# A second level of Strassen inside three products of q, k and v

## The chip, the cores and the metric

The kernel runs on one NeuronCore of a Trainium2 chip. The metric is device time in microseconds (us) of one execution; the times below are medians over runs. TensorE multiplies matrices into PSUM (eight banks of 128 partitions by 512 float32), VectorE and ScalarE read PSUM, GpSimd works on SBUF alone, and transfers are queued on SyncE.

## The reference

Two layers over 64 graphs of 256 nodes with 512 features, with one shared 256x256 adjacency. All values are float32.

```
h = relu(layernorm(x));   x = x + (adj @ h) @ W0 + b0                  # layer 0
h = relu(layernorm(x))                                                  # layer 1: 8 heads of 64
q, k, v = h @ Wq + bq, h @ Wk + bk, h @ Wv + bv
a = softmax(q k^T / 8 + (1 - adj) * -1e9)
x = x + (a v) @ Wo + bo
```

## The kernel before, in words

Work goes in 32 groups of two batches (512 tokens). A first loop over groups runs layer 0 and leaves the residual and the hidden state in DRAM; a second loop runs layer 1.

Every dense product (W0, Wq, Wk, Wv, Wo) of a group is done by one level of Strassen's algorithm in the Winograd form, with seven block products in place of eight. The two column halves of the operand are the group's two batches. `weight_sums` (L405) makes the sums of weight quarters once, `Halves.sums` (L433) makes the sums of activation quarters (t1 to t4) for each group on GpSimd, `product` (L439) issues one block product, and `project` (L447) the seven of them. A block product is four matmuls of 128x128 weights over 256 columns into one bank; each shows as two TensorE instructions in the profile. `project` keeps a running sum in bank `pa`: a11 b11, then + s2 t2, then + s3 t3. `read` takes the state of a bank out before more is added to it (on ScalarE for q, k and v; for W0 and Wo it is an add on VectorE), and `finish` adds a bank and such a partial result into a target with one VectorE add (`add`, L492). The order of products is a11, a12, s2, s1, s3, a22, s4.

Banks are handed out by hand, first in, first out (`bank`, `give`): a bank that is given back goes to the end of the list of free ones, and whoever takes it waits for its last reader. Partial results u have three buffers in turn (`partial`, L489).

The order of the second loop (from L816) for each group g is: `attend(g, 0)`, `score(g, 1)`, `queries_keys(g+1)`, `attend(g, 1)`, `score(g+1, 0)`, `values(g+1)`, `post(g)`. Each engine takes its instructions in the order in which they are issued. `score` (L684) makes scores for two head groups and two batches: four pairs of banks, which VectorE scales and masks into SBUF (L699, eight instructions); GpSimd subtracts a row maximum (L705), ScalarE takes the exponential (L710), and GpSimd adds keys (L717). `attend` (L719) makes denominators (`pden`) and the weighted values (`pav`, two banks); VectorE takes reciprocals (L743) and, one step later, divides (L750), which frees these two banks. `post` (L661) is the product with Wo; its `read` (L667) and `finish` (L671) add into the residual on VectorE.

Side work is put off with `after(delay, ...)` to later steps; `tick` (called at every `yield` of a running product sequence) issues what is due. So a GpSimd sum given with delay 2 enters GpSimd's queue two products later. `hidden_sums` (L619) does so for t1 to t4 of the hidden state, during `post`.

Of the kernel before, what the change touches and what calls it, by code (L numbers as in the profile page):

```python
# [8 lines left out]
F32 = mybir.dt.float32  # L9
I32 = mybir.dt.int32  # L10
AF = mybir.ActivationFunctionType
ALU = mybir.AluOpType
AX = mybir.AxisListType
P = 128
# [7 lines left out]
def load_weight(nc, pool, w, name):  # L22
    t = pool.tile([P, w.shape[0] // P, w.shape[1]], F32, name=name)
    nc.sync.dma_start(t, w.rearrange("(c p) o -> p c o", p=P))
    return t


def load_row(queue, pool, b, name):
    t = pool.tile([P, b.shape[0]], F32, name=name)
    queue.dma_start(t, bass.AP(tensor=b.tensor, offset=b.offset, ap=[[0, P], [1, b.shape[0]]]))  # L30
    return t
# [167 lines left out]
def kernel(  # L199
# [16 lines left out]
    nc = tc.nc  # L216
    B, N, D = x.shape
    H, HD = 8, D // 8
    DC = D // P
    NT = N // P  # L220
    GB = 2
# [12 lines left out]
    const = main.enter_context(tc.tile_pool(name="const", bufs=1))  # L234
    dram = main.enter_context(tc.tile_pool(name="between", bufs=1, space=bass.MemoryType.DRAM))
    xpool = main.enter_context(tc.tile_pool(name="x", bufs=4))
    act = main.enter_context(tc.tile_pool(name="act", bufs=1))
# [8 lines left out]
    def bank(shape, name):  # L246
        i = free_banks.pop(0)
        t = psum.tile(shape, F32, tag=f"bank{i}", name=name)
        bank_of[id(t)] = (i, t)
        return t  # L250

    def give(t):
        free_banks.append(bank_of.pop(id(t))[0])
# [5 lines left out]
    def after(delay, fn, *args):  # L259
        entered[0] += 1  # L260
        later.append((clock[0] + delay, entered[0], fn, args))
# [8 lines left out]
    X, H0, Q, K, V, OT = {}, {}, {}, {}, {}, {}  # L270
# [18 lines left out]
    def quarter(xt, i, k):  # L289

        return xt[:, k * NT:(k + 1) * NT, i * HF:(i + 1) * HF]
# [11 lines left out]
    b0_r = load_row(nc.scalar, const, b0, "b0_r")  # L303
    w0_sb = load_weight(nc, const, w0, "w0_sb")
# [8 lines left out]
    adjT = const.tile([P, NT, N], F32, name="adjT")  # L313
# [89 lines left out]
    W = {}  # L403
# [16 lines left out]
    class Halves:  # L420

        def __init__(self, name, tokens, which):
            self.tokens = tokens
            self.t = {n: act.tile([P, 2, N], F32, tag=f"{n}{which}", name=f"{n}_{name}")
                      for n in ("t1", "t2", "t3", "t4")}

        def operand(self, n, c=slice(0, 2)):
            if n[0] == "t":
                return self.t[n][:, c, :]
            j, k = int(n[1]) - 1, int(n[2]) - 1  # L430
            return self.tokens[k][:, 2 * j:2 * j + 2, :][:, c, :]

        def sums(self, eng, which=("t1", "t2", "t3", "t4"), c=slice(0, 2)):  # L433
            args = {"t1": ("b12", "b11"), "t2": ("b22", "t1"), "t3": ("b22", "b12"), "t4": ("b21", "t2")}
            for n in which:
                p, q = args[n]
                eng.tensor_tensor(self.t[n][:, c, :], self.operand(p, c), self.operand(q, c), op=ALU.subtract)  # L437

    def product(ps, s, a, halves, b, by_token, start=True, stop=True):  # L439
        for m in range(2):  # L440
            for c in range(2):
                w, y = s[a][:, c, :], halves.operand(b, c)
                lhs, rhs = (y[:, m * P:(m + 1) * P], w) if by_token else (w[:, m * P:(m + 1) * P], y)
                nc.tensor.matmul(ps[:, m, :], lhs, rhs, start=(start and m + c == 0), stop=(c == 1),  # L444
                                 skip_group_check=True)

    def project(s, halves, by_token, name, read, finish, first_half_first=False):  # L447


        def new(n):  # L450
            return bank([P, 2, N], f"{name}{n}")
        pa = new("a")
        product(pa, s, "a11", halves, "b11", by_token, stop=False)
        u1 = read(pa, 1)
        yield
        if first_half_first:
            pc = new("c")
            product(pc, s, "s1", halves, "t1", by_token, stop=False)
            c22 = read(pc, 0)
            yield  # L460
        pb = new("b")
        product(pb, s, "a12", halves, "b21", by_token)
        finish(pb, u1, 0, 0)
        give(pb)
        yield
        product(pa, s, "s2", halves, "t2", by_token, start=False, stop=False)
        u2 = read(pa, 2)
        yield
        if not first_half_first:
            pc = new("c")  # L470
            product(pc, s, "s1", halves, "t1", by_token, stop=False)
            c22 = read(pc, 0)
            yield
        product(pa, s, "s3", halves, "t3", by_token, start=False)
        u3 = read(pa, 3)
        finish(pa, c22, 1, 1)
        give(pa)
        yield
        pd = new("d")
        product(pd, s, "a22", halves, "t4", by_token)  # L480
        finish(pd, u3, 1, 0)
        give(pd)
        yield
        product(pc, s, "s4", halves, "b22", by_token, start=False)
        finish(pc, u2, 0, 1)
        give(pc)
        yield

    def partial(name, n):  # L489
        return tmp.tile([P, 2, N], F32, tag="u", name=f"u{n}_{name}")  # L490

    def add(o, ps, u):  # L492
        nc.vector.tensor_tensor(o, ps, u, op=ALU.add)  # L493
# [113 lines left out]
    H1T, HH, HO = {}, {}, {}  # L607
# [11 lines left out]
    def hidden_sums(g, *steps):  # L619

        HH[g] = Halves(f"h_{g}", [H1T[g][:, k] for k in range(GB)], 0 if g else 1)
        for step, n in zip(steps, ("t1", "t2", "t3", "t4")):
            after(step, HH[g].sums, nc.gpsimd, (n,))

    def queries_keys(g):

        for n, store in (("q", Q), ("k", K)):
            store[g] = {}
            bias = L1[n][1]

            def read(ps, m):
                u = partial(f"{n}_{g}", m)
                for c in range(2):
                    f = 2 * (m in (0, 3)) + c
                    nc.scalar.activation(u[:, c, :], ps[:, c, :], AF.Identity, bias=bias[:, f:f + 1])
                return u

            def finish(ps, u, i, k):
                o = store[g][i, k] = act.tile([P, 2, N], F32, tag=f"{n}{i}{k}", name=f"{n}_{g}_{i}{k}")
                add(o, ps, u)  # L640

            yield from project(W[n], HH[g], False, f"{n}_{g}", read, finish)

    def values(g):
        v = act.tile([P, HQ, GB, NT, HF], F32, tag="yT0", name=f"v_{g}")
        V[g] = {(i, k): v[:, i, k] for i in range(HQ) for k in range(GB)}

        def read(ps, m):
            u = partial(f"v_{g}", m)
            nc.scalar.copy(u, ps)  # L650
            return u

        def finish(ps, u, i, k):
            add(V[g][i, k], ps, u)

        yield from project(W["v"], HH.pop(g), True, f"v_{g}", read, finish)

    def quarter_of(batch, i):
        return batch.rearrange("(t p) d -> p t d", p=P)[:, :, i * HF:(i + 1) * HF]

    def post(g):  # L661

        xt = X.pop(g)
        halves = HO.pop(g)
        done = []

        def read(ps, n):  # L667
            o = quarter(xt, *RESIDUAL[n])
            add(o, ps, o)

        def finish(ps, u, i, k):  # L671
            o = quarter(xt, i, k)
            add(o, ps, o)
            done.append(k)
            if g == NG - 1:
                nc.sync.dma_start(quarter_of(out[g * GB + k], i), o)
            elif done.count(k) == 2:
                nc.sync.dma_start(out[g * GB + k].rearrange("(t p) d -> p t d", p=P), xt[:, k * NT:(k + 1) * NT, :])

        yield from project(W["o"], halves, True, f"o_{g}", read, finish, first_half_first=g == NG - 1)  # L680
# [82 lines left out]
    def run(gen, steps=99):  # L763

        for _ in zip(range(steps), gen):
            tick()
# [46 lines left out]
    run(steps)  # L813
    hidden_sums(1, 1, 2, 8, 9)
    run(values(0))
    for g in range(NG):  # L816
        attend(g, 0)
        load_residual(g)
        if g + 2 < NG:
            load_hidden(g + 2)  # L820
        score(g, 1, 5)
        tick()
        for t in range(T):
            after(9 + t, lambda t, xt: nc.gpsimd.tensor_tensor(xt[:, t, :], xt[:, t, :], L1["o"][1], op=ALU.add), t, X[g])  # L824
        if g + 1 < NG:
            run(queries_keys(g + 1))
        else:
            run(post(g - 1))
        attend(g, 1)
        if g + 1 < NG:  # L830
            score(g + 1, 0, 5)
            tick()
            run(values(g + 1))
            if g + 2 < NG:
                hidden_sums(g + 2, 2, 3, 4, 5)
                run(post(g))
    tick()
    last = post(NG - 1)
# [45 lines left out]
```

## Time and profile before

| what | value |
|---|---|
| median of 3 runs | 2727.9 us (2727.74 to 2728.13) |
| profiled span | 2725.3 us |
| VectorE's masked scores (L699), 512 | 312.1 us busy, 683 ns each |
| GpSimd's subtraction (L705), 254 | 593.7 us busy, 2373 ns each |
| VectorE's reciprocals (L743), 256 | 216.8 us busy, 909 ns each |
| mean granted TensorE clock | 0.998 of full speed |

In the profile, PE is TensorE's matmuls and PEld its weight loads, DVE is VectorE, ACT is ScalarE, POOL is GpSimd. A line of a timeline gives the start and the length in us, the engine, the line of the kernel, the instruction with its output and inputs, its shape and how many are merged into the line; in brackets stands how long the engine had been idle and who ended that. Durations of neighbours can overlap: an engine takes the next instruction before the last one's results are out.

### The profile page before, as it was taken

Reading aid. Unit: us, or ns where it says so; the run is one execution under the profiler, and the core shown is the slowest. Engines: PE = TensorE matmul, PEld = TensorE weight load, DVE = VectorE, ACT = ScalarE, POOL = GpSimd, SP = SyncE. Lnnn points to the kernel's source line nnn. Section 1 sums busy time; section 2 is a strip of 40 time slices with the busy share of each in tenths; the row PEclk is TensorE's granted clock in tenths of the full one; section 3 lists DMA queues with packets and bytes.
Section 4 is the critical chain, followed back from the end, with each engine's and each line's share of the span. In section 5 each row is a group of like instructions: output and inputs, shape, how many; then the busy total and the mean of one; then the engine's idle time right before and its main releaser. Section 6 shows DMA issues by size and latency. Waiting matters only on the chain.

```text
span 2725.3 us, 43511 instructions
## 1 busy us (share of the span) xinstructions
PE 2699.5 (99%) x17172; PEld 2252.1 (83%) x17172; DVE 1539.6 (56%) x2781; ACT 874.2 (32%) x1537; POOL 1823.1 (67%) x1426
## 2 busy tenths in 40 slices
PE   8999999999999999999999999999999999999998
PEld 7888888888788888888888888888888888888886
DVE  7877778775444444455554444454555445444556
ACT  3434343443233223222233322222223332223222
POOL 6777776764666666666666666666666666666665
PEclk9999999999999999999999999999999999999999
DMA  7776666664111111111111111111222111111110
GB/s 187 188 193 163 162 168 169 165 153 93 47 47 47 47 47 47 47 47 47 47 47 47 47 47 47 47 47 56 61 62 57 48 47 47 47 47 47 47 47 32
DMA packets 281023, 210.50 MB, mean 77 GB/s; under 512 B 145904, under 2 KB 212976, under 8 KB 280816
## 3 DMA queue, kind: packets, MB, share of 16 engines
q1 hardware_dynamic: 280352, 207.15, 29.2%
q8 instruction: 138, 2.26, 0.4%
q10 hardware_dynamic: 464, 0.52, 0.1%
q14 instruction: 69, 0.57, 0.1%
HBM read 106.96 MB, written 100.66 MB: 76 GB/s over the span
## 4 chain that ended last, share of the span: by engine, by line
PE 98%; POOL 1%; DVE 1%; DMA 0%; issue 0%; ACT 0%; DVEq 0%; ACTq 0%; POOLq 0%
PE sc L694 8%; PE py L539 8%; PE pav L733 8%; PE pden L726 2%; POOL a L705 1%; PE v_31a L444 0%; PE q_31a L444 0%; PE q_27a L444 0%; PE v_22a L444 0%; PE v_18a L444 0%; PE q_18a L444 0%; PE q_14a L444 0%; PE v_9a L444 0%; PE v_5a L444 0%; PE q_5a L444 0%; PE v_30a L444 0%
## 5 line engine op out<-in xcount | busy, mean ns | idle before, releaser
L705 POOL TENSOR_TENSOR a<-a,top 128x1024 f32<-128x1024 f32 x254 | 593.7, 2373 | 699.1 <-DVE a L699 699.1
L699 DVE SCALAR_TENSOR_TENSOR a<-sc,maskT 128x512 f32<-128x512 f32 x512 | 312.1, 683 | 28.5 <-PE sc L694 28.5
L717 POOL TENSOR_TENSOR as<-a 128x512 f32<-128x512 f32 x256 | 317.3, 1277 | 0.7 <-DVE r L575 0.7
L710 ACT ACTIVATE a<-a 128x1024 f32<-128x1024 f32 x256 | 270.8, 1058 | 22.4 <-POOL a L705 22.4
L743 DVE RECIPROCAL den<-den 128x128 f32<-128x128 f32 x256 | 216.8, 909 | 66.9 <-ACT den L740 66.8
L694 PE MATMUL sc<-q,k 64*128 64x256 f32 x2048 | 238.7, 383 | 0.0
L733 PE MATMUL pav<-a,v 128*32 128x256 f32 x4096 | 232.7, 379 | 0.0
L694 PEld LDWEIGHTS sc<-q,k 64*128 64x128 f32 x2048 | 194.4, 187 | 44.9 <-issue 26.3
L539 PE MATMUL py<-adjT,h 128*128 128x256 f32 x1024 | 228.9, 382 | 0.9 <-DVE adjT L325 0.9
L740 ACT ACTIVATE den<-pden 128x512 f32<-128x512 f32 x64 | 38.2, 597 | 581.7 <-PE pden L726 570.6
L539 PEld LDWEIGHTS py<-adjT,h 128*128 128x128 f32 x1024 | 196.1, 192 | 28.7 <-ACT h L514 1.2
L733 PEld LDWEIGHTS pav<-a,v 128*32 128x32 f32 x4096 | 133.1, 110 | 87.9
L569 ACT ACTIVATE h<-x,nb,rs 128x512 f32<-128x512 f32 x128 | 97.1, 806 | 319.0 <-POOL nb L54 319.0
L824 POOL TENSOR_TENSOR x<-x,bo_r 128x512 f32<-128x512 f32 x128 | 159.4, 1283 | 12.9 <-DVE x L493 12.9
L53 POOL TENSOR_TENSOR rs<-rs,mhalf 128x2 f32<-128x2 f32 (+1 forms) x97 | 78.8, 812 | 124.3 <-DVE nb L52 124.2
L518 POOL TENSOR_TENSOR x<-x,b_r 128x512 f32<-128x512 f32 x128 | 159.3, 1280 | 1.0 <-ACT h L514 0.9
L437 POOL TENSOR_TENSOR t_y<-yT,t_y 128x256 f32<-128x256 f32 (+1 forms) x96 | 87.8, 915 | 41.5 <-ACT yT L549 39.0
L752 ACT ACTIVATE den<-den 128x512 f32<-128x512 f32 x64 | 40.3, 630 | 221.5 <-DVE den L743 221.5
L590 DVE BATCH_NORM_STATS2 st<-x 128x6 f32<-128x256 f32 x256 | 96.4, 418 | 4.4
L514 ACT ACTIVATE h<-x,nb,rs 128x512 f32<-128x512 f32 x128 | 93.9, 805 | 10.5 <-POOL nb L54 10.5
L42 DVE BATCH_NORM_STATS2 st<-x 128x6 f32<-128x512 f32 x128 | 85.6, 669 | 7.2 <-DMA x<-in_x_dram 7.2
L437 POOL TENSOR_TENSOR t_y<-yT 128x256 f32<-128x256 f32 (+1 forms) x96 | 87.6, 912 | 2.2 <-ACT yT L549 0.9
(3144 smaller groups left out, 5550.1 us busy)
## 6 DMA issues: line engine op xcount, KB each, us to landing
x<-in_x_dram SPq DMA_DIRECT2D x256, 128.0 KB, 3.5
residual<-x SPq DMA_DIRECT2D x256, 128.0 KB, 2.3
hidden<-r SPq DMA_DIRECT2D x128, 256.0 KB, 4.7
h1T<-hidden SPq DMA_DIRECT2D x64, 512.0 KB, 9.5
x<-residual SPq DMA_DIRECT2D x32, 1024.0 KB, 6.5
out_dram<-x SPq DMA_DIRECT2D x62, 512.0 KB, 3.0
w_sb<-in_L_gnn_weight_dram SPq DMA_DIRECT2D x1, 1024.0 KB, 6.3
wq_sb<-in_L_gnn_Wq_dram SPq DMA_DIRECT2D x1, 1024.0 KB, 6.8
```

The costliest lines, as they stand in the source:

```text
L437: eng.tensor_tensor(self.t[n][:, c, :], self.operand(p, c), self.operand(q, c), op=ALU.subtract)
L518: nc.gpsimd.tensor_tensor(xt[:, t, :], xt[:, t, :], b0_r, op=ALU.add)
L539: nc.tensor.matmul(pss[d][:, b * N:(b + 1) * N], h[:, b * NT + k, d * P:(d + 1) * P], adjT[:, k, :], start=(k == 0), stop=(k == NT - 1))
L569: nc.scalar.activation(h1[:, k * NT + t, :], xt[:, k * NT + t, :], AF.Relu, bias=nb[:, t:t + 1], scale=rs[:, t:t + 1])
L694: nc.tensor.matmul(ps[j][:, kt * N:(kt + 1) * N], k[j * HD:(j + 1) * HD, c, kt * P:(kt + 1) * P], q[j * HD:(j + 1) * HD, c, :], start=True ...
L699: nc.vector.scalar_tensor_tensor(a[:, j * NT:(j + 1) * NT, :].rearrange("p k n -> p (k n)"), ps[j], SCALE, maskT_f, op0=ALU.mult, op1=ALU.add)
L705: nc.gpsimd.tensor_tensor(a, a, top_b, op=ALU.subtract)
L710: nc.scalar.activation(a, a, AF.Exp)
L717: nc.gpsimd.tensor_tensor(AS[c, b], a4[:, :, 0, :], a4[:, :, 1, :], op=ALU.add)
L733: nc.tensor.matmul(po[f][h * 32:(h + 1) * 32, b * N:(b + 1) * N], v[:, k, h * HD + f * 32:h * HD + f * 32 + 32], A[h // 2, b][:, (h % 2) * ...
L743: nc.vector.reciprocal(rden[:, c * P:(c + 1) * P], den[:, c * P:(c + 1) * P])
L824: after(9 + t, lambda t, xt: nc.gpsimd.tensor_tensor(xt[:, t, :], xt[:, t, :], L1["o"][1], op=ALU.add), t, X[g])
```

## The change

From group 4 on, three of the seven block products of each of q, k and v, those whose result is used once only (`a12 b21`, `a22 t4`, `s4 b22`), are themselves done by a second level of the same algorithm: seven matmuls of 128x128 over 128 columns in place of four over 256. It is for fewer TensorE columns per product. Four of the seven go to one quarter of the result each, three or four are needed in several quarters and go to a bank `shared`; VectorE then adds the quarters together (`finish2`). For `s4`, which accumulates onto bank `pc`, the fourth shared product can't go straight into the quarter c22.

The operands' sums come from GpSimd: for the weights once, in the first three groups of the second loop (`block_sums`, into the space of layer 0's weights), for the activations in each group (`block_hidden`, steps 6 and 7 of `post`). The order of products becomes a11, s1, s2, a12, s3, a22, s4.

```diff
+    def product2(own, shared, s, x, by_token, fresh):
+        q = own.rearrange("p m (n k) -> p (m n) k", k=P)
+        c11, c12, c21, c22 = (q[:, i, :] for i in ((0, 2, 1, 3) if by_token else (0, 1, 2, 3)))
+        for o, a, b, start in ((shared[:, 0, :], "a11", "b11", True), (shared[:, 1, :], "s2", "t2", False),
+                               (shared[:, 2, :], "s3", "t3", False),
+                               (c22 if fresh else shared[:, 3, :], "s1", "t1", fresh),
+                               (c11, "a12", "b21", False), (c12, "s4", "b22", False), (c21, "a22", "t4", False)):
...
+            nc.tensor.matmul(o, lhs, rhs, start=start, stop=True, skip_group_check=True)
+
+    def finish2(o, own, shared, u, by_token, fresh):
...
+        add(o, own, u)
+        q = quarters(o)
+        lower = q[:, 1::2, :] if by_token else q[:, 2:4, :]
+        right = q[:, 2:4, :] if by_token else q[:, 1::2, :]
+        add(q, spread(0, 4), q)
+        add(q[:, 1:4, :], spread(1, 3), q[:, 1:4, :])
+        add(lower, spread(2, 2), lower)
+        if fresh:
+            add(right[:, 0, :], quarters(own)[:, 3, :], right[:, 0, :])
+        else:
+            add(right, spread(3, 2), right)
+
+    def project2(n, halves, blocks, by_token, name, read, target):
...
+        def once(own, a, i, k, u, fresh):
+            shared = bank([P, 4, P], f"{name}r")
+            product2(own, shared, W2[n, a], blocks[ONCE[a]], by_token, fresh)
+            finish2(target(i, k), own, shared, u, by_token, fresh)
...
+        pa = new("a")
+        product(pa, s, "a11", halves, "b11", by_token, stop=False)
+        u1 = read(pa, 1)
+        yield
+        pc = new("c")
+        product(pc, s, "s1", halves, "t1", by_token, stop=False)
+        c22 = read(pc, 0)
+        yield
+        product(pa, s, "s2", halves, "t2", by_token, start=False, stop=False)
+        u2 = read(pa, 2)
+        yield
+        once(new("b"), "a12", 0, 0, u1, True)
+        yield
+        product(pa, s, "s3", halves, "t3", by_token, start=False)
+        u3 = read(pa, 3)
+        add(target(1, 1), pa, c22)
+        give(pa)
+        yield
+        once(new("d"), "a22", 1, 0, u3, True)
+        yield
+        once(pc, "s4", 0, 1, u2, False)
+        yield
...
-            yield from project(W[n], HH[g], False, f"{n}_{g}", read, finish)
+            if g < FIRST2:
+                yield from project(W[n], HH[g], False, f"{n}_{g}", read, finish)
+            else:
+                yield from project2(n, HH[g], H2[g], False, f"{n}_{g}", read, target)
...
-        yield from project(W["v"], HH.pop(g), True, f"v_{g}", read, finish)
+        if g < FIRST2:
+            yield from project(W["v"], HH.pop(g), True, f"v_{g}", read, finish)
+        else:
+            yield from project2("v", HH.pop(g), H2.pop(g), True, f"v_{g}", read, lambda i, k: V[g][i, k])
...
+        if g < 3:
+            for i, work in enumerate(block_sums("qkv"[g])):
+                after(4 + i // 2, *work)
...
                 hidden_sums(g + 2, 2, 3, 4, 5)
+                if g + 2 >= FIRST2:
+                    block_hidden(g + 2, 6)
                 run(post(g))
```

More of the change, by code (lines that the diff above doesn't have):

```diff
@@ L487, in project, with block_sums, part @@
         yield
+    ONCE = {"a12": "b21", "a22": "t4", "s4": "b22"}
+    FIRST2 = 4
+    W2, spare = {}, []
+    def block_sums(n):
+        todo = []
+        for a in ONCE:
+            w = W[n][a]
+            def part(i, j):
+                return w[:, j, i * P:(i + 1) * P]
+            s1, s2, s3, s4 = (spare.pop(0) for _ in range(4))
+            W2[n, a] = dict(a11=part(0, 0), a12=part(0, 1), a22=part(1, 1), s1=s1, s2=s2, s3=s3, s4=s4)
+            for o, p, q, op in ((s1, part(1, 0), part(1, 1), ALU.add), (s2, s1, part(0, 0), ALU.subtract),
+                                (s3, part(0, 0), part(1, 0), ALU.subtract), (s4, part(0, 1), s2, ALU.subtract)):
+                todo.append((nc.gpsimd.tensor_tensor, o, p, q, op))
+        return todo
@@ new lines, with __init__, operand, sums @@
+    class Blocks:
+        def __init__(self, x, t):
+            self.x, self.t = x, t
+        def operand(self, n):
+            if n[0] == "t":
+                return self.t[..., {"t1": 0, "t3": 1, "t2": 2, "t4": 3}[n], :]
+            return self.x[..., int(n[1]) - 1, int(n[2]) - 1, :]
+        def sums(self, eng):
+            t, op = self.t, ALU.subtract
+            eng.tensor_tensor(t[..., 0:2, :], self.x[..., :, 1, :], self.x[..., 0, :, :], op=op)
+            eng.tensor_tensor(t[..., 2, :], self.operand("b22"), t[..., 0, :], op=op)
+            eng.tensor_tensor(t[..., 3, :], self.operand("b21"), t[..., 2, :], op=op)
@@ new lines, in product2 @@
+    def product2(own, shared, s, x, by_token, fresh):
[5 more added lines that the diff above has]
+                               (c11, "a12", "b21", False), (c12, "s4", "b22", False), (c21, "a22", "t4", False)):
+            lhs, rhs = s[a], x.operand(b)
+            if by_token:
+                lhs, rhs = rhs, lhs
+            nc.tensor.matmul(o, lhs, rhs, start=start, stop=True, skip_group_check=True)
@@ new lines, in finish2, with quarters, spread @@
+    def finish2(o, own, shared, u, by_token, fresh):
+        def quarters(t):
+            return t.rearrange("p m (n k) -> p (m n) k", k=P)
+        def spread(i, n):
+            return shared[:, i:i + 1, :].to_broadcast([P, n, P])
+        add(o, own, u)
[9 more added lines that the diff above has]
+            add(right, spread(3, 2), right)
@@ new lines, in project2, with new @@
+    def project2(n, halves, blocks, by_token, name, read, target):
+        s = W[n]
+        def new(i):
+            return bank([P, 2, N], f"{name}{i}")
+        def once(own, a, i, k, u, fresh):
+            shared = bank([P, 4, P], f"{name}r")
+            product2(own, shared, W2[n, a], blocks[ONCE[a]], by_token, fresh)
+            finish2(target(i, k), own, shared, u, by_token, fresh)
+            give(own)
+            give(shared)
+        pa = new("a")
[20 more added lines that the diff above has]
+        yield
@@ L623, in hidden_sums, with block_hidden @@
             after(step, HH[g].sums, nc.gpsimd, (n,))
+    H2 = {}
+    def block_hidden(g, step):
+        t = act.tile([P, GB, 4, P], F32, tag="t2", name=f"t2_{g}")
+        t4 = act.tile([P, 4, P], F32, tag="t24", name=f"t24_{g}")
+        x = H1T[g][:, :, 2:4, :].rearrange("p k c (n j) -> p k c n j", j=P)
+        both = Blocks(x, t)
+        last = Blocks(HH[g].t["t4"].rearrange("p c (n j) -> p c n j", j=P), t4)
+        H2[g] = {f"b2{k + 1}": Blocks(x[:, k], t[:, k]) for k in range(GB)}
+        H2[g]["t4"] = last
+        after(step, both.sums, nc.gpsimd)
+        after(step + 1, last.sums, nc.gpsimd)
     def queries_keys(g):
@@ L636, in read, with target @@
                 return u
+            def target(i, k):
+                o = store[g][i, k] = act.tile([P, 2, N], F32, tag=f"{n}{i}{k}", name=f"{n}_{g}_{i}{k}")
+                return o
             def finish(ps, u, i, k):
-                o = store[g][i, k] = act.tile([P, 2, N], F32, tag=f"{n}{i}{k}", name=f"{n}_{g}_{i}{k}")
-                add(o, ps, u)
-            yield from project(W[n], HH[g], False, f"{n}_{g}", read, finish)
+                add(target(i, k), ps, u)
+            if g < FIRST2:
+                yield from project(W[n], HH[g], False, f"{n}_{g}", read, finish)
+            else:
+                yield from project2(n, HH[g], H2[g], False, f"{n}_{g}", read, target)
     def values(g):
@@ L824 @@
             after(9 + t, lambda t, xt: nc.gpsimd.tensor_tensor(xt[:, t, :], xt[:, t, :], L1["o"][1], op=ALU.add), t, X[g])
+        if g == 0:
+            for n, tag in ((4 * DC, "w0_sb"), (4, "w0_s1"), (4, "w0_s2"), (4, "w0_s4"), (4, "adjT"), (4, "b0_r")):
+                t = const.tile([P, n, P], F32, tag=tag, name=f"spare_{tag}")
+                spare.extend(t[:, i, :] for i in range(n))
+        if g < 3:
+            for i, work in enumerate(block_sums("qkv"[g])):
+                after(4 + i // 2, *work)
         if g + 1 < NG:
```

## The prediction, made blind

> **What bounds the kernel now.** I read the page first: engine totals, then the chain that ended last.
>
> ```profile
> PE 2699.5 (99%) x17172; PEld 2252.1 (83%) x17172; DVE 1539.6 (56%) x2781; ACT 874.2 (32%) x1537; POOL 1823.1 (67%) x1426
> ...
> PE 98%; POOL 1%; DVE 1%; DMA 0%; issue 0%; ACT 0%; DVEq 0%; ACTq 0%; POOLq 0%
> ```
>
> TensorE is never idle and carries 98% of the chain. So anything taken from it is worth its full time, as long as nobody else then makes it wait. VectorE is busy for only 56% of the span, but that is an average; I read the stretch where the change puts its work. One group of two batches takes two half-periods of about 32.5 us (attend, score and fourteen products each). In the timeline (start, duration, engine, line, what) TensorE and then VectorE show:
>
> ```profile
> 1514.21 1.89 PE L444 MATMUL o_12c<-wo_s,oT 128*128 128x256 f32 x8
> 1516.03 1.07 PE L726 MATMUL pden<-as,ones 128*32 128x256 f32 x16
> 1516.91 3.64 PE L733 MATMUL pav<-a,v 128*32 128x256 f32 x64
> 1520.48 3.72 PE L694 MATMUL sc<-q,k 64*128 64x256 f32 x32
> 1524.13 1.99 PE L444 MATMUL q_14a<-h1T,wq_sb 128*128 128x256 f32 x8
> 1525.96 1.89 PE L444 MATMUL q_14b<-h1T,wq_sb 128*128 128x256 f32 x8
> 1527.69 1.89 PE L444 MATMUL q_14a<-t_h,wq_s 128*128 128x256 f32 x8
> ```
> ```profile
> 1516.13 0.69 DVE L493 TENSOR_TENSOR x<-o_12c,x 128x512 f32<-128x512 f32 x1 [1.03 <-PE o_12c L444]
> 1517.88 3.39 DVE L743 RECIPROCAL den<-den 128x128 f32<-128x128 f32 x4 [1.06 <-ACT den L740]
> 1521.71 4.88 DVE L699 SCALAR_TENSOR_TENSOR a<-sc,maskT 128x512 f32<-128x512 f32 x8 [0.44 <-PE sc L694]
> 1526.51 1.28 DVE L750 TENSOR_TENSOR oT<-pav,den 128x512 f32<-128x512 f32 x2
> ```
>
> A product is eight TensorE instructions (a float32 matmul is two); products follow each other at 1.73 us, 0.216 us an instruction. VectorE is free of its products when attend begins, starts the reciprocals 1.86 us into it and the eight masked scores (L699) 5.7 us into it. These have only 0.44 us of slack; eight take 4.88 us, so one starts every 0.60 us.
>
> **The Trainium skill.** "TensorE: Matmul & The Clock Gate", LDWEIGHTS, puts a load at columns/1.2 ns, 107 ns for 128. Its Back-to-back issue gap section warns that in load-and-matmul pairs both set the pace (81 ns at 128 columns against 56 alone). The change's 128-column matmuls come nearest to the four transposes in the mask set-up, each with its own 128-column load:
>
> ```profile
> 416.96 0.60 PE L341 MATMUL pm<-ident,adj_sb 128*128 128x128 f32 x4
> 417.39 0.81 PE L539 MATMUL py<-adjT,h 128*128 128x256 f32 x3
> ```
>
> Four instructions of 0.272 us each (the tile's own view) span 0.60 us, so (0.60 - 0.272)/3 = 0.109 us apart, half of the 0.216. So here the load fits under a matmul of 128 columns, just.
>
> "VectorE: DVE Perf Modes", The DRAIN you can't avoid, says that order alone doesn't make a read of the result just written safe; a semaphore is wanted. The trace has such pairs:
>
> ```profile
> 412.59 0.69 DVE L42 BATCH_NORM_STATS2 st<-x 128x6 f32<-128x512 f32 x1
> 413.31 0.18 DVE L43 BATCH_NORM_AGGREGATE mv<-st 128x2 f32<-128x6 f32 x1
> ```
>
> The reader starts 0.03 us after the writer's end, while independent instructions start 0.08 us before it (0.60 apart at 0.69). [...] Length I take from the same page's errata section, (N+151)/0.96 ns: 0.691 for 512 (trace 0.69), so estimates of 0.557 for 384, 0.424 for 256 and 0.291 for 128. "GPSIMD Engine Reference", Specifications, has GpSimd contend with VectorE instructions of two SBUF inputs; the new adds have one input in PSUM, like L493, which holds 0.69 beside a busy GpSimd.
>
> **The change, part by part.** It acts in 28 groups (4 to 31), on three products of each of q, k and v: 252 in all.
>
> TensorE: eight instructions of 256 columns become seven matmuls, 14 instructions, of 128. 8 x 0.216 = 1.727 us become 14 x 0.1092 = 1.529; 0.198 saved. Per group 9 x 0.198 = 1.78 us, in all 50 us. That is the whole gain.
>
> VectorE: one add of 0.69 becomes five adds, each reading what the one before wrote. Fresh bank: 0.69 + 0.69 + 0.557 + 0.424 + 0.291 plus four gaps of 0.034, less 0.084 overlap with the next: F = 2.70 us. For s4 the last add is on 256: 2.84. A whole project2 has 2.70 + 0.60 + 2.70 + 2.84 = 8.85 us of VectorE work where there were about 2.5.
>
> It can't begin before the first once-product ends, for the order puts three plain products ahead. Call that moment 0. TensorE then does s3 (1.73), a22 (3.26), s4 (4.79) and is done. VectorE starts 0.27 later (1527.96 against 1527.69 above), and its inputs are there each time: 0.27 + 2.70 = 2.97; add for (1,1) to 3.58; a22 to 6.28; s4 to 9.12. It ends 4.34 us behind TensorE. After q this costs nothing: three plain products of k follow, VectorE is idle by then and the banks in rotation are free. It costs in two places.
>
> Place A, after k: attend and score follow. Queued behind the last add are the reciprocals, then the eight L699. The reciprocals start 4.34 us into attend, not 1.86; with the 0.44 of slack used up, L699 starts 2.05 us late. Score writes eight banks; three are held by attend until L750 or given back just before, so that its last pair takes the banks of its first. Before, these came free just in time (second L699 ends at 1521.71 + 0.60 + 0.69 = 1523.0; the pair is due at 1523.1). So the 2.05 us go to TensorE. K's last quarter is ready 4.4 us into attend, before score's second pair wants it: no cost there.
>
> Place B, after v: post follows. Its first read (L667) adds bank pa to the residual on VectorE, and s2 accumulates into pa only after that. The read now ends at 9.12 + 0.69 = 9.81; s2 is due at 4.79 + 2 x 1.727 = 8.24, and needs some 0.07 for the semaphore and 0.107 for its load: 9.99. TensorE waits 1.75 us. In group 31 no post follows; attend wants V instead, with about the same wait. Later adds of post catch up, as VectorE has 1 us of idle time at each product there.
>
> GpSimd: block sums per group are one 512-, three 256- and two 128-wide operations: 1.28 + 3 x 0.73 + 2 x about 0.45 (estimate, from 1.28 and 0.73) = 4.4 us. In the half-period with post it ends its hidden sums at 1578.5 and idles for 9.5 us until the next scores: hidden there. The 36 weight-block sums (5.5 us in each of three groups) delay key sums by less than the some 8 us until attend. ScalarE keeps its reads, a step earlier for one; copies wait behind the same exponentials as before. New tiles add no DMA.
>
> Sum per group: 2.05 + 1.75 - 1.78 = 2.02 us; 28 x 2.02 = 56 us, on 2727.9: 2784.
>
> **Rivals.** (1) *Five adds that close up.* If each add starts 0.08 us before the end of the one before, F falls by 4 x 0.118 = 0.47, the lag by 1.42, the waits to 0.63 and 0.33: (0.96 - 1.78) x 28 = -23, 2705, faster. For it: independent adds do so. Against: these depend on each other and the trace holds such pairs apart. (2) *VectorE's lag is hidden altogether*: 50 us saved, 2678, faster. For it: only 56% busy. Against: the slack at A is 0.44 us. (3) *Weight loads become the bound.* At the break-even 1.727/14 = 0.123 us a load nothing is saved on a product; the lag shrinks by 2 x 0.198, waits of 1.65 and 1.35 stay: +84, 2812, slower still. At the 0.142 us that one transpose load lasts: 2.0 us a product, +0.26 each on nine, waits 1.1 and 0.8: +119, 2847. For it: "PEld" is 83% busy, and the skill's 81 against 56. Against: 0.109 in the transposes.
>
> **How the numbers follow.** Main case 0.62, (1) 0.14, (2) 0.10, (3) 0.14. In the main case F is uncertain by about 0.15 us, one more semaphore step or one less per add; three of F in each of two waits and 28 groups make 25 us either way. Faster are (1), (2) and a sliver of the main case: 0.25; slower 0.72; same 0.03. The range leaves out most of (2) and the upper end of (3): 2698 to 2825.
>
> **What would show it.** In the trace after: new matmuls 0.109 us apart; five adds in about 2.8 us; reciprocals some 4.3 us after attend begins; a hole of about 2 us before score's last pair, ended by L699's line, and one of 1.7 us before post's s2, ended by VectorE's read; VectorE near 2050 us busy (252 x about 1.96 = 494 more). I'm wrong if VectorE catches up before attend and post, or if the matmuls come slower than 0.12.

## The result, and the profile after

The changed kernel takes 2771.5 us (median; 2769.2 to 2772.0) where the kernel before takes 2728.0: a ratio of 1.0156, 95% interval 1.0138 to 1.0173. It is slower by 43.5 us; the forecast was slower by 56.

The page of the changed kernel, totals and then the chain that ended last:

```profile
PE 2690.7 (97%) x18684; PEld 2271.7 (82%) x18684; DVE 2002.4 (72%) x3789; ACT 875.6 (32%) x1537; POOL 1961.6 (71%) x1630
...
PE 67%; POOL 17%; DVE 14%; issue 1%; DMA 0%; POOLq 0%; ACT 0%; DVEq 0%; SPq 0%; ACTq 0%
```

TensorE's share of the chain fell from 98% to 67%. VectorE is 463 us busier, 1.84 us for each of the 252 products. The chain also names GpSimd at 17%; whether that is a cause has to be tested. First, the stretch where the forecast put its two waits. A once-product here is one of the three products of q, k or v whose result is used once only, and a hole is a stretch in which TensorE waits. TensorE in the changed kernel, from k's first once-product to post (start, duration, engine, line, what; in brackets idle time and who ended it):

```profile
1554.59 0.38 PE L538 MATMUL k_14r<-h1T,wk_sb 128*128 128x128 f32 x2
...
1556.15 1.89 PE L444 MATMUL k_14a<-t_h,wk_sb 128*128 128x256 f32 x8
...
1561.10 1.07 PE L856 MATMUL pden<-as,ones 128*32 128x256 f32 x16
1561.98 3.64 PE L863 MATMUL pav<-a,v 128*32 128x256 f32 x64
1565.55 2.86 PE L824 MATMUL sc<-q,k 64*128 64x256 f32 x24
1569.03 1.72 PE L824 MATMUL sc<-q,k 64*128 64x256 f32 x8 [0.62 <-DVE a L829]
1570.69 1.99 PE L444 MATMUL v_14a<-wv_sb,h1T 128*128 128x256 f32 x8
...
1584.12 1.89 PE L444 MATMUL o_13b<-wo_sb,oT 128*128 128x256 f32 x8
1587.27 1.97 PE L444 MATMUL o_13a<-wo_s,t_o 128*128 128x256 f32 x8 [1.26 <-DVE x L600]
```

The same places in the kernel before:

```profile
1548.51 1.07 PE L726 MATMUL pden<-as,ones 128*32 128x256 f32 x16
...
1556.61 1.99 PE L444 MATMUL v_14a<-wv_sb,h1T 128*128 128x256 f32 x8
...
1570.53 1.89 PE L444 MATMUL o_13b<-wo_sb,oT 128*128 128x256 f32 x8
1572.26 1.89 PE L444 MATMUL o_13a<-wo_s,t_o 128*128 128x256 f32 x8
```

Both holes are where they were forecast: at score's last eight instructions (place A), ended by VectorE's masked scores, and before post's s2 (place B), ended by VectorE's read. From attend to the first product of v took 1570.69 - 1561.10 = 9.59 us, where the kernel before needs 1556.61 - 1548.51 = 8.10: 1.49 us. Half of that lies before the eight instructions and half among them, where TensorE waits for the second of the two banks that they write. Post's s2 was due 1.73 after 1584.12 and started 1.42 later.

VectorE in the same stretch:

```profile
1556.42 0.69 DVE L600 TENSOR_TENSOR k<-k_14b,u_k 128x512 f32<-128x512 f32 x1 [2.88 <-PE k_14b L538]
1557.15 1.74 DVE L600 TENSOR_TENSOR k<-k_14r,k 128x512 f32<-128x512 f32 x3
1558.81 0.28 DVE L600 TENSOR_TENSOR k<-k_14b,k 128x128 f32<-128x128 f32 x1
1559.00 0.68 DVE L600 TENSOR_TENSOR k<-k_14a,u_k 128x512 f32<-128x512 f32 x1
1559.64 0.69 DVE L600 TENSOR_TENSOR k<-k_14d,u_k 128x512 f32<-128x512 f32 x1
1560.37 1.74 DVE L600 TENSOR_TENSOR k<-k_14r,k 128x512 f32<-128x512 f32 x3
1562.03 0.28 DVE L600 TENSOR_TENSOR k<-k_14d,k 128x128 f32<-128x128 f32 x1
1562.22 0.68 DVE L600 TENSOR_TENSOR k<-k_14c,u_k 128x512 f32<-128x512 f32 x1
1562.94 2.20 DVE L600 TENSOR_TENSOR k<-k_14r,k 128x512 f32<-128x512 f32 x4
1565.06 3.38 DVE L873 RECIPROCAL den<-den 128x128 f32<-128x128 f32 x4
1568.35 4.81 DVE L829 SCALAR_TENSOR_TENSOR a<-sc,maskT 128x512 f32<-128x512 f32 x8
```

From 1556.42 to the end of these lines VectorE waits for nobody. The reciprocals start 3.96 us into attend (before: 1.86), the masked scores 7.25 (before: 5.7).

The distance from one attend to the next gives a balance without any modelling. It is read off the starts of `pden` in TensorE's timeline. Each half-period begins with an attend and a score; one goes on with q and k, the other with v and post, and the latter has both holes.

| kernel | half with q and k, us | half with v and post, us | time, us |
|---|---|---|---|
| before | 32.48 | 32.48 | 2728.0 |
| changed | 31.50 | 34.97 | 2771.5 |
| TensorE's part alone | 31.50 | 31.99 | 2687.0 |
| VectorE's part alone | 32.48 | 35.13 | 2803.4 |
| q only | 31.99 | 32.48 | 2713.1 |
| v only | 32.48 | 33.49 | 2758.1 |
| order of before, second level | 31.50 | 34.97 | 2772.5 |
| order of after, one level | 32.48 | 32.48 | 2728.3 |
| spread once-products | 31.50 | 32.85 | 2711.3 |
| spread, last of k and v at one level | 31.66 | 32.15 | 2697.9 |
| reciprocals late | 31.50 | 33.49 | 2731.1 |
| other order in post | 31.50 | 34.58 | 2761.6 |
| both of these | 31.50 | 33.10 | 2723.3 |
| both, on the kernel before | 32.48 | 33.59 | 2761.3 |

So six second-level products save 0.98 us and three save 0.49, 0.164 each, and the two holes together are 34.97 - 31.99 = 2.98 us (1.49 each; in post 1.42 before s2 and 0.07 in s2 itself, which is followed 1589.07 - 1587.27 = 1.80 us later where 1.73 is usual). 28 x (2.98 - 1.47) = 42 us.

### The profile page after: what moved, and what is told of

Its sections match the earlier page's. It is cut to its first block, busy times and chain, and to the rows that moved or that the text cites. A ratio compares the mean times of both kernels' runs of the same rounds, so it can differ in the third digit from the quotient of the medians.

```text
span 2769.3 us, 47852 instructions
## 1 busy us (share of the span) xinstructions
PE 2690.7 (97%) x18684; PEld 2271.7 (82%) x18684; DVE 2002.4 (72%) x3789; ACT 875.6 (32%) x1537; POOL 1961.6 (71%) x1630
## 4 chain that ended last, share of the span: by engine, by line
PE 67%; POOL 17%; DVE 14%; issue 1%; DMA 0%; POOLq 0%; ACT 0%; DVEq 0%; SPq 0%; ACTq 0%
POOL a L835 10%; DVE k L600 9%; PE py L646 8%; PE sc L824 5%; PE pav L863 4%; POOL as L847 4%; DVE den L873 4%; POOL t_o L437 3%; PE pden L856 1%; DVE a L829 1%; DVE x L600 1%; DVE v L600 0%; PE q_27a L444 0%; PE q_25a L444 0%; PE q_19a L444 0%
## 5 line engine op out<-in xcount | busy, mean ns | idle before, releaser
L824 PE MATMUL sc<-q,k 64*128 64x256 f32 x2048 | 262.8, 387 | 17.4 <-DVE a L829 17.4
L840 ACT ACTIVATE a<-a 128x1024 f32<-128x1024 f32 x256 | 264.6, 1057 | 23.9 <-POOL a L835 23.9
```

What stands on the lines that cost most here:

```text
L824: nc.tensor.matmul(ps[j][:, kt * N:(kt + 1) * N], k[j * HD:(j + 1) * HD, c, kt * P:(kt + 1) * P], q[j * HD:(j + 1) * HD, c, :], start=True ...
L840: nc.scalar.activation(a, a, AF.Exp)
```

## The experiments

The theory is the lag, the time by which VectorE ends its adds after TensorE has gone on to attend or post: TensorE is faster, VectorE isn't done when attend and post begin, and what is queued behind it makes TensorE wait. The rivals are GpSimd (17% of the chain), the order of products, and the narrow matmuls themselves.

**Each engine's part alone.** First the four added adds are left out, so the shared products don't enter the result:

```diff
         add(o, own, u)
...
-        add(q, spread(0, 4), q)
-        add(q[:, 1:4, :], spread(1, 3), q[:, 1:4, :])
-        add(lower, spread(2, 2), lower)
-        if fresh:
-            add(right[:, 0, :], quarters(own)[:, 3, :], right[:, 0, :])
-        else:
-            add(right, spread(3, 2), right)
```

> TensorE's part alone. The changed kernel with the last four of the five adds left out, so that the shared products are computed on TensorE but never enter the result (the output isn't the reference's); GpSimd's block sums and the order of products stay. Lag theory: VectorE again ends 0.6 us after each product, both holes (before score's last pair, before post's third product) are gone, and what is left is nine products a group that are 1.727 - 1.56 = 0.165 us shorter: 2728 - 28 x 9 x 0.165 = 2686 us. Rival, GpSimd: the chain in the changed kernel runs 17% over GpSimd, and its extra sums make the holes; then these stay and the time is near 2771.

Measured: 2687.0 us, ratio 0.9849 (0.9833 to 0.9866), with GpSimd's extra sums all made. TensorE has 98% of the chain again, and no hole is left. So the narrow matmuls and GpSimd's sums cost nothing by themselves, and the saving is real: 41 us.

Then VectorE's adds with TensorE's old products:

```diff
-            shared = bank([P, 4, P], f"{name}r")
-            product2(own, shared, W2[n, a], blocks[ONCE[a]], by_token, fresh)
-            finish2(target(i, k), own, shared, u, by_token, fresh)
+            product(own, s, a, halves, ONCE[a], by_token, start=fresh)
+            finish2(target(i, k), own, own.rearrange("p m (n k) -> p (m n) k", k=P), u, by_token, fresh)
```

> VectorE's part alone. The changed kernel with each once-product made again by four matmuls of 256 columns, followed by the same five adds, which read the product's own bank in place of the shared one (the output isn't the reference's); GpSimd's sums and the order stay. Lag theory: VectorE's 8.9 us from the first once-product run against 3 x 1.727 = 5.2 us of TensorE in place of 4.85, so the lag and each hole shrink by 0.33 us: holes of 1.49 - 0.33 = 1.16 and 1.42 - 0.33 = 1.09 us, nothing saved: 2728 + 28 x 2.25 = 2791 us. Rival, narrow matmuls themselves (their waits, weight loads, banks) cause the loss: near 2728.

Measured: 2803.4 us, ratio 1.0273 (1.0256 to 1.029). The sign and place are as forecast, the size is 12 us above. VectorE's timeline of this run shows why:

```profile
1640.38 0.68 DVE L598 TENSOR_TENSOR k<-k_15a,u_k 128x512 f32<-128x512 f32 x1
1641.18 0.69 DVE L598 TENSOR_TENSOR k<-k_15d,u_k 128x512 f32<-128x512 f32 x1
...
1646.60 3.38 DVE L871 RECIPROCAL den<-den 128x128 f32<-128x128 f32 x4
```

The adds of a22 start 0.80 us after the add before, not 0.64: they wait for their product, which ends later than in the changed kernel. So the lag shrinks by 0.16 us (reciprocals 3.80 us into attend, which began at 1642.80), not by the 0.33 that the slower products would give alone. Holes of 1.49 - 0.16 = 1.33 each make 28 x 2.66 = 74 us; the half-period shows 35.13 - 32.48 = 2.65.

**The order of products.** Once undone at two levels, once alone at one level:

```
project2 of the changed kernel:   a11, s1, s2, a12, s3, a22, s4
second level, order of before:    a11, a12, s2, s1, s3, a22, s4
one level, order of after:        a11, s1, s2, a12, s3, a22, s4
```

> The order of products undone: second level and five adds as in the changed kernel, but products in the order of the kernel before (a11, a12, s2, s1, s3, a22, s4). Lag theory: from the end of s3 VectorE does the add for (1,1), waits for a22 (1.56 + 0.27 = 1.83 us), then 2.58 + 2.84 us, so it ends at 7.25 us against TensorE's 3.12: a lag of 4.13 us where the changed kernel has 4.06. So the order hardly matters: 2770 to 2775 us. Rival, the new order is what hurts: 2728 - 41 = 2687 or at least well below 2760.

> The order of products alone: one level everywhere (four matmuls of 256 columns and one add for each product of q, k and v), in the changed kernel's order, with GpSimd's block sums still made though nobody reads them. Lag theory: VectorE ends about 0.9 us after each product sequence as before, no hole: 2728 us, within 2. Rivals, order or GpSimd's sums cost time by themselves: above 2735.

Measured: 2772.5 us (ratio 1.0161, 1.0144 to 1.0178) and 2728.3 us (ratio 1.0000, 0.9992 to 1.0009). The order chosen neither helps nor hurts; the second run also clears GpSimd's block sums once more.

**Which of q, k and v.**

For q alone, k goes back to one level in `queries_keys` and v in `values`; for v alone, `queries_keys` gets the `if True` and `values` stays as it is. The cut shows the two lines of the first run:

```diff
-            if g < FIRST2:
+            if g < FIRST2 or n == "k":
...
-            if g < FIRST2:
+            if True:
```

> The second level for q alone; k and v at one level in the old order. After q three plain products of k follow, in which VectorE can catch up, and neither attend nor post comes next. Lag theory: no hole, and 28 x 3 x 0.165 = 14 us saved: 2714 us. Rival, loss in proportion to the number of second-level products: 2728 + 43.5 x 3/9 = 2742 us.

> The second level for v alone; q and k at one level. Lag theory: the hole after k is gone, the one in post stays at 1.42 us: 2728 + 28 x (1.42 - 3 x 0.165) = 2754 us. If GpSimd's key sums end that hole (they are later in the changed kernel because score is delayed after k), then it shrinks to nothing here, as score isn't delayed any more: 2714 us. Loss in proportion to products: 2742.

Measured: 2713.1 us (ratio 0.9945, 0.9928 to 0.9961) and 2758.1 us (ratio 1.0108, 1.0091 to 1.0125). The same second level gains 15 us in q and loses 30 in v: what follows decides. TensorE in v alone, at post:

```profile
1645.63 1.89 PE L444 MATMUL o_14b<-wo_sb,oT 128*128 128x256 f32 x8
1648.78 1.97 PE L444 MATMUL o_14a<-wo_s,t_o 128*128 128x256 f32 x8 [1.26 <-DVE x L600]
```

It is the same idle time as in the changed kernel, with score no longer delayed. So the hole in post doesn't come from the one in score.

**Where VectorE's work lies.** The same nine second-level products and all the adds, in another order, so that the adds of a12 lie beside s1 and s2:

```
project2 of the changed kernel:   a11, s1, s2, a12, s3, a22, s4
once-products spread:             a11, a12, s1, s2, s4, s3, a22
```

> The changed kernel with the once-products spread: a11, a12, s1, s2, s4, s3, a22. The adds of a12 lie beside s1 and s2; from the end of s4 VectorE does 0.27 + 2.84 + 0.64 + 2.58 = 6.33 us against TensorE's 1.73 + 1.56 = 3.29, a lag of 3.04 in place of 4.06. Lag theory: holes of 0.47 and 0.40 us, so 2728 + 28 x (0.87 - 1.48) = 2711 us, faster than before. Rival, the work on VectorE as a whole counts, not where it lies: no change, 2771.

And the last product of k and v back at one level:

```diff
-        once(new("d"), "a22", 1, 0, u3, True)
+        if n == "q":
+            once(new("d"), "a22", 1, 0, u3, True)
+        else:
+            pd = new("d")
+            product(pd, s, "a22", halves, "t4", by_token)
+            add(target(1, 0), pd, u3)
+            give(pd)
```

> As the run with spread once-products, but the last product of k and of v (a22) is made at one level again, so that seven of nine products a group have the second level. From the end of s4 VectorE does 0.27 + 2.84 + 0.64 + 0.60 = 4.35 us against TensorE's 3.45: a lag of 0.9 us, as in the kernel before. Lag theory: no hole, 28 x 7 x 0.165 = 32 us saved: 2696 us, below both kernels. If some other cost goes with the second level: above 2728.

Measured: 2711.3 us (ratio 0.9937, 0.992 to 0.9954) and 2697.9 us (ratio 0.989, 0.9874 to 0.9907). Both match, and both beat the kernel before. The first has VectorE just as busy as the changed kernel:

```profile
PE 2678.9 (99%) x18684; PEld 2274.2 (84%) x18684; DVE 2006.3 (74%) x3789; ACT 875.5 (32%) x1537; POOL 1962.0 (72%) x1630
```

VectorE's busy time is unchanged but for 4 us (2006), and 60 us have gone from the kernel's time. In the second, VectorE and then TensorE before and in attend:

```profile
1597.20 2.20 DVE L606 TENSOR_TENSOR k<-k_15r,k 128x512 f32<-128x512 f32 x4
1599.32 0.68 DVE L606 TENSOR_TENSOR k<-k_15a,u_k 128x512 f32<-128x512 f32 x1
1599.92 0.68 DVE L606 TENSOR_TENSOR k<-k_15d,u_k 128x512 f32<-128x512 f32 x1
1601.62 3.39 DVE L879 RECIPROCAL den<-den 128x128 f32<-128x128 f32 x4 [1.02 <-ACT den L876]
```
```profile
1599.76 1.07 PE L862 MATMUL pden<-as,ones 128*32 128x256 f32 x16
1600.64 3.64 PE L869 MATMUL pav<-a,v 128*32 128x256 f32 x64
1604.21 3.72 PE L830 MATMUL sc<-q,k 64*128 64x256 f32 x32
1607.87 1.99 PE L444 MATMUL v_15a<-wv_sb,h1T 128*128 128x256 f32 x8
```

VectorE is idle again for 1.02 us before the reciprocals, which start 1.86 us into attend as before, and attend to v takes 8.11 us. TensorE is back at 98% of the chain. GpSimd does the same work in the same order after score as in the changed kernel, and no hole is left in post: its 17% of the chain was no cause. Nor was a shortage of banks: the bank `shared` is taken for seven of the nine products here too, and both half-periods are shorter by the full 0.164 us for each of them.

**The queue at place A and the read at place B, each by itself.** In the first of these runs the reciprocals go behind the masked scores on VectorE:

```diff
+        late = qd == 1 and g < NG - 1
+        def turn():
+            for c in range(4):
+                nc.vector.reciprocal(rden[:, c * P:(c + 1) * P], den[:, c * P:(c + 1) * P])
+        if not late:
+            turn()
...
         def divide():
+            if late:
+                turn()
...
+            if late:
+                after(5, count)
```

> Place A alone mended, by VectorE's queue. In the changed kernel the reciprocals of attend's second half, 3.3 us between the late adds and the masked scores, are issued after the masked scores, and ScalarE's count on them five steps later. Everything else stays, the lag of 4 us too. If the queue in front of the masked scores makes the hole: they start some 4 us into attend, the hole of 1.49 us before score's last pair goes, the one in post stays: 2771.5 - 28 x 1.49 = 2730 us. If score waits for something else (K's last quarter, GpSimd): no gain.

Measured: 2731.1 us (ratio 1.0012, 1.0003 to 1.002), 40 us gained by a change of order alone. VectorE:

```profile
1612.81 2.20 DVE L600 TENSOR_TENSOR k<-k_15r,k 128x512 f32<-128x512 f32 x4
1616.66 4.88 DVE L829 SCALAR_TENSOR_TENSOR a<-sc,maskT 128x512 f32<-128x512 f32 x8 [1.65 <-PE sc L824]
1621.46 3.38 DVE L876 RECIPROCAL den<-den 128x128 f32<-128x128 f32 x4
```

The lag is still there (attend began at 1610.97, the last add ends 4.0 us later), but the masked scores now wait for score, not score for them. The half-period with v and post is 1.48 us shorter. The hole at A was the queue, not K's last quarter.

For place B one more product was put between post's first product and its s2:

```diff
-        yield from project(W["o"], halves, True, f"o_{g}", read, finish, first_half_first=g == NG - 1)
+        yield from project(W["o"], halves, True, f"o_{g}", read, finish, first_half_first=True)
```

> Place B alone mended, by one product more ahead of the wait. In the changed kernel post makes s1 before a12, so that TensorE has three products after v, not two, before it needs VectorE's first read of pa: due at 4.85 + 3 x 1.727 = 10.03 us after the first once-product of v, while VectorE has read it at about 9.8. If that read makes the hole: 2771.5 - 27 x 1.5 = 2731 us. If GpSimd's key sums end it: no gain.

The other two runs have this edit and the late reciprocals together, one in the changed kernel and one in the kernel before.

> Both places mended, all nine once-products a group at the second level, all five adds made. If the two holes are all that the second level costs, what stays is TensorE's saving: 2771.5 - 42 - 40 = 2689 us, near the run of TensorE's part alone (2687) and below the best so far (2698). If the holes only move elsewhere: above 2698.

> The two remedies in the kernel before, without any second level. It has no hole in either place: 2728 us, within 3. If the remedies gain by themselves: below 2720.

Measured: 2761.6 us (ratio 1.0124, 1.0107 to 1.0141), 2723.3 us (0.9982, 0.9976 to 0.9989) and 2761.3 us (1.0122, 1.0105 to 1.0139). The forecasts for these three missed by 30 us or more, all by the same cause, which the third run shows best, since it has no second level at all:

```profile
1587.35 1.89 PE L444 MATMUL o_13a<-wo_s,t_o 128*128 128x256 f32 x8
1590.11 1.97 PE L444 MATMUL o_13a<-wo_sb,t_o 128*128 128x256 f32 x8 [0.87 <-DVE x L493]
```

The hole before s2 is gone, as expected. But in this order s2 and s3 follow each other into the same bank, and s3 has to wait for VectorE's read between them: 1.03 us from the due time, 1.11 in the half-period. The order holds in every group's post, 30 of them in such half-periods: 30 x 1.11 = 33 us, which is what the third run lost. In the other two the same two products are just as far apart (2.76 and 2.77 us). The remedy was badly made; it took the wait away in one place and made one in another. With that subtracted, both remedies together would stand at 2723.3 - 33 = 2690 (an estimate), near TensorE's part alone, but a post order free of both waits was not run.

## Why the prediction was right

The direction, the places and the mechanism were right; the sizes were too large. The gain was put 9 us too high and the loss 23 us, and the two errors cancel in part, so that the total came nearer than its terms.

- *TensorE saves 0.198 us a product.* Mis-sized: 0.164. The fourteen instructions take 1556.15 - 1554.59 = 1.56 us, 0.111 each, not the 0.109 of the four transposes. Saved: 41 us (run with TensorE's part alone), not 50.
- *F = 2.70 us for a fresh bank.* Mis-sized: 1559.00 - 1556.42 = 2.58. The error is one of reading the program: the fifth add was said to read what the fourth wrote. It works on another quarter, so it starts 0.08 us before the end of the one before (1558.81 against 1557.15 + 1.74), where 0.034 after it had been counted: 0.12 us. For s4, where each add does depend on the one before, 2.84 was forecast and 1565.06 - 1562.22 = 2.84 measured. The Trainium skill ("VectorE: DVE Perf Modes", The DRAIN you can't avoid) says that order alone doesn't make a read of a result just written safe and that a semaphore does. It gives no time for that; the trace has dependent adds 0.03 to 0.04 us after the end of the one before (1557.15 after 1556.42 + 0.69). Rival (1) fell for the dependent adds.
- *VectorE lags by 4.34 us.* Mis-sized: 3.96. The adds take 1565.06 - 1556.15 = 8.91 us from the end of the first once-product, not 9.12 (twice 0.12 less for F, 0.04 more for the single add), and attend starts 4.95 us after it, not 4.79. Of this 0.06 comes from the slower matmuls; the other 0.10 is the step from the last product to attend, which the forecast left out although its lines show it (1516.03 - 1514.21 = 1.82, where products follow at 1.73).
- *Place A, 2.05 us.* Mis-sized: 1.49. The lag is 0.38 smaller. The slack was 0.54, not 0.44: with nothing to wait for, the masked scores start 3.29 us after the reciprocals (1568.35 - 1565.06), and before it was 1521.71 - 1517.88 = 3.83. So they start 1.57 us late, and 0.08 of that is absorbed before it reaches TensorE.
- *Place B, 1.75 us.* Mis-sized: 1.42 to the start of s2, and 0.07 more while it runs. The read ends 9.59 us after v's first once-product, not 9.81 (that product ended at 1577.53, the read at 1586.44 + 0.68); s2 was due at 8.32, not 8.24; and it started 0.15 after the read, where about 0.18 had been allowed.
- *About the same wait in group 31's attend.* It is 1.13 us there, once: from attend to score 2717.99 - 2712.41 = 5.58 us, before 2677.64 - 2673.19 = 4.45.
- *q costs nothing, GpSimd costs nothing, copies on ScalarE cost nothing.* Right: q alone gains 15 us, and the half-period with q and k has the whole saving of its six products. GpSimd's 138 us more busy time (forecast 28 x 4.4 + 3 x 5.5 = 140) show in no half-period.
- *Sum 28 x 2.02.* 28 x 1.51 by the half-periods.

Rival (2), a lag that is hidden altogether, fell in the changed kernel; the run with the last products at one level shows what it takes to hide it. Rival (3), weight loads as the bound, fell: 0.111 us an instruction, where 0.123 would have been break-even.

The chain of waits would have misled here. At place B of the changed kernel it reads (start, duration, what):

```profile
1582.73 3.70 POOL as L847 x3
1586.44 0.69 DVE x L600
1587.13 0.14 issue
1587.27 1.97 PE o_13a L444 x8
```

It takes GpSimd's key sums for what released VectorE's read at 1586.44. VectorE's own timeline shows no gap in front of that read:

```profile
1584.32 2.20 DVE L600 TENSOR_TENSOR v<-v_14r,v 128x512 f32<-128x512 f32 x4
1586.44 0.68 DVE L600 TENSOR_TENSOR x<-o_13a,x 128x512 f32<-128x512 f32 x1
```

The read starts 0.08 us before the end of the add in front of it, as a read that waits for nothing does; the key sum merely ended at that moment. The run with the last products at one level has the same GpSimd work and no hole.

## What to carry to other kernels

In this kernel, work that was moved from the bounding engine to a half-idle one was paid for where the two met next, not in the average. So ask what is queued behind it on that engine and how soon the bounding engine needs it. The same five adds cost nothing where three plain products follow (q) and more than the whole saving where attend or post comes next (k, v). Three things helped when the helper lagged: to spread its work, to put what others wait for further ahead in its queue, and to keep the cheap form for the last step. The first and the third together turned a loss of 43 us into a gain of 30, with the same idea. And a remedy that makes one wait go away has to be followed to the next use of the same bank.

## What the runs showed of the hardware that was not expected

A float32 matmul of 128 columns with its own 128-column weight load keeps a pace of 0.111 us in a stream, 3% more than half of the 0.216 us for 256 columns. The Trainium skill ("TensorE: Matmul & The Clock Gate", Back-to-back issue gap) has 81 ns at 128 columns for a stream in which each matmul brings its load, against 56 for a matmul alone, and names no type there. That let one expect a larger loss; in float32, as here, no run shows one.
